# Selective-scan layer of a four-layer network: the product with B moves from TensorE and VectorE to GpSimd, and the side work is cut into evenly spaced items

## The chip, the cores and the metric

The kernel runs on one core of one Trainium2 chip, all in fp32. The metric is device time in microseconds of one launch. A core has five engines that run their own instruction queues in order: PE (TensorE), DVE (VectorE), ACT (ScalarE), POOL (GpSimd) and SP, which here only issues DMAs. They meet through semaphores.

## The reference

Four layers follow each other on four images of 128 channels and 48 x 48 pixels. Only layer 0 is changed; layers 1 to 3 (a deformable convolution, linear attention, two expert layers, softmax attention) stay as they are.

Layer 0 normalises the tokens, projects them to 256 channels, applies a depthwise 3 x 3 convolution and SiLU (call the result u), and then runs a selective scan in four directions k over the 2304 tokens, with 16 states n per channel:

```python
def step(h, inp):
    u_t, d_t, B_t, C_t = inp
    dA = jnp.exp(d_t[..., None] * A)
    h = h * dA + (d_t * u_t)[..., None] * B_t[:, :, None, :]
    y = jnp.einsum('bkdn,bkn->bkd', h, C_t)
    return (h, y)
```

Here d_t is a softplus of a small projection of u, and B_t and C_t are projections of u with one value per token and state. The four directions are summed, D * u is added, and the sum is normalised, gated with SiLU(z), projected back to 128 channels and added to the input.

## The kernel before, in words

**Tiling.** The 256 channels lie as two halves d of 128 partitions. The tokens of a direction are cut into three chunks of 768, so an image has 12 pieces (`PIECES`) and the four images have 48. A piece has 16 steps, one for each state n, so the loop at the end of `_layer0` runs over 768 steps g. The recurrence of one step is done by one scan instruction along the 768 tokens for each half (`scan`, L449).

**A step.** These are the operations, and the engine of each:
- `spread` (L415, L426): POOL makes dB, for each block of 128 tokens a diagonal matrix that holds B of this state (affine_select); SP loads rB, the same 768 values of B broadcast over all partitions, from DRAM.
- `decay` (L431): ACT makes dA = exp(delta * A) for each half.
- `times_b` (L435): PE multiplies duT (delta * u of half 0, turned to tokens by channels) with dB, twelve instructions here (six blocks; the profile counts two for each fp32 product), into the PSUM tile b0. This is the input of half 0.
- `scan` (L444, L449): DVE multiplies du of half 1 with rB into h, and then scans both halves: the first takes b0 from PSUM, the second h from SBUF, in place.
- `keep` (L461): POOL copies the last column of h as the start of the next chunk.
- `turn` (L467, L474): PE turns h to tokens by channels; ACT scales each token by C into hs.
- `back` (L482): PE turns hs back and adds it up over the 16 states in the PSUM tile yp.
- `collect` (L504, L513): after a piece, DVE adds yp to y in SBUF.

The steps are staggered: in step g the scan of g runs, `turn` and `back` of g - 1, `decay` and `times_b` of g + 1, `spread` of g + 2.

**Side work.** `prepare` makes delta, du, duT and the rows of B and C for the next piece (L321 to L393); `pre` normalises and convolves the next image (`before`, `convolve`), `post` finishes the last one (`after`, `offsets`), and `columns` (L282, POOL) copies u column by column. They stand in lists of closures, `urgent` and `others`. `fill` takes one or two from the front of them at three places of a step, so that the side work stands in the first half of a piece or so, and the list is emptied at some borders.

**What sets the order.** Instructions of PE, ACT, DVE and POOL are issued in the order of the code (`manual_schedule`), so each engine's queue holds the step's operations and the side work in the order in which this loop calls them. PSUM is shared by a pool of three tiles for all passing results, b0 (two banks) and yp (three banks). In SBUF most tiles have two buffers, rB three.

Of the kernel before, what the change touches and what calls it, by code (L numbers as in the profile page):

```python
# [23 lines left out]
P = 128  # L24
# [76 lines left out]
TPC = CH // P  # L101
HB = BLK // 2


def _layer0(ctx, env, dr, io, table, offs):
# [9 lines left out]
    ps = ctx.enter_context(tc.tile_pool(name="l0p", bufs=3, space=PSUM))  # L115
# [7 lines left out]
    def psum(*shape):  # L123
        return ps.tile(list(shape), F32, name="ps", tag="ps")
# [15 lines left out]
    bo = load("l1_bo", [NOFF, 1])  # L140

# [25 lines left out]

    b0 = py.tile([P, 2, 512], F32, name="b0").rearrange("p b f -> p (b f)")[:, :CH]
    yp = py.tile([P, ND * CH // 512, 512], F32, name="yp")
    yp = yp.rearrange("p b f -> p (b f)").rearrange("p (d f) -> p d f", d=ND)  # L170

    bank = [(d * CH + m * P) // 512 for m in range(TPC) for d in range(ND)]

# [3 lines left out]
    def taps(pp, weights, pad, r):  # L177

        for t in range(TAPS):
            nc.tensor.matmul(  # L180
                pp,
                weights[:, t, :],
                pad[:, 4 * r + t // 3 : 4 * r + t // 3 + 4, t % 3 : t % 3 + HW],
                start=t == 0,
                stop=t == TAPS - 1,
            )
# [4 lines left out]
    def standardise(x):  # L191
# [13 lines left out]
        def second():  # L205
            for g in range(G3):
                nc.vector.tensor_scalar(
                    x[:, g, :],
                    x[:, g, :],
                    mv[:, g, 0:1],  # L210
                    rstd[:, g : g + 1],
                    op0=ALU.subtract,
                    op1=ALU.mult,
                )
# [11 lines left out]

    def before(im, j):
# [8 lines left out]
        def turn():  # L236
            pt = psum(P, G3, C)
            for g in range(G3):
                nc.tensor.transpose(pt[:, g, :], t["xb"][:, bass.ts(g, P)], ident)
            t["xt"] = sp.tile([P, G3, C], F32, name="xt")  # L240
            nc.scalar.copy(t["xt"], pt)
            t["first"], t["second"] = standardise(t["xt"])

        def back():
            pt = psum(P, BLK)
            for g in range(G3):
                nc.tensor.transpose(pt[:, bass.ts(g, P)], t["xt"][:, g, :], ident)
            t["xn"] = sp.tile([P, BLK], F32, name="xn")
            nc.scalar.activation(t["xn"], pt, AF.Identity, bias=ln_b, scale=ln_g)
            nc.sync.dma_start(im.xn[:, cols], t["xn"])  # L250

        def project(d):
            pp = psum(P, BLK)
            nc.tensor.matmul(pp, ipT[:, bass.ts(d, P)], t["xn"], start=True, stop=True)
            nc.vector.tensor_copy(rows_of(pads[d], j), by_row(pp))
# [3 lines left out]
            turn,  # L259
            lambda: t["first"](),  # L260
            lambda: t["second"](),
            back,
            lambda: project(0),
            lambda: project(1),
        ]

    def convolve(d, r):

        pp = psum(P, HB)
        taps(pp, diag[:, d], pads[d], r)  # L270
        nc.scalar.activation(
            u_hw[:, d, bass.ts(r, HB)], pp, AF.Identity, bias=cb[:, d : d + 1]
        )
# [21 lines left out]

    def pre(im):
        steps = merged([before(im, j) for j in range(NBLK)], 3)
        convs = [lambda d=d, r=r: convolve(d, r) for r in range(L // HB) for d in range(ND)]
        return steps + convs + [activate]
# [8 lines left out]
    def prepare(x, before_it):  # L308
# [7 lines left out]
        def project(s):  # L316
            if s == 0:
                t["xd"] = sp.tile([NR + NS, CH], F32, name="xd", bufs=1)
            pp = psum(NR + NS, BLK)
            for d in range(ND):  # L320
                nc.tensor.matmul(  # L321
                    pp,
# [5 lines left out]
            nc.scalar.copy(t["xd"][:, bass.ts(s, BLK)], pp)  # L328
# [4 lines left out]
        def tokens():  # L333

            pp = psum(P, TPC, 2 * NS)
            for m in range(TPC):
                for d in range(ND):
                    nc.tensor.matmul(
                        pp[:, m, :],
# [4 lines left out]
                    )  # L344
            x.bc = sp.tile([P, TPC, 2 * NS], F32, name="bct")
            nc.vector.tensor_copy(x.bc, pp)


        def raw(s, d):
            if s == 0 and d == 0:  # L350
# [3 lines left out]
            pp = psum(P, BLK)  # L354
            nc.tensor.matmul(
                pp, dtT[:, k, bass.ts(d, P)], t["xd"][:NR, sub], start=True, stop=True
            )
            bias = dtb[:, d, k : k + 1]
            nc.scalar.activation(t["e"][:, d, sub], pp, AF.Abs, bias=bias)
            nc.vector.tensor_scalar(x.delta[:, d, sub], pp, bias, 0.0, op0=ALU.add, op1=ALU.max)  # L360

        def exps(d):
            nc.scalar.activation(t["e"][:, d, :], t["e"][:, d, :], AF.Exp, scale=-1.0)

        def rest(d):
            r = sp.tile([P, CH], F32, name=f"du{d}", bufs=1 + d)
            t["r", d] = r
            nc.vector.tensor_scalar(r, t["e"][:, d, :], 1.0, -1.0, op0=ALU.add, op1=ALU.add)
            nc.vector.scalar_tensor_tensor(
                r, r, -1.0, t["e"][:, d, :], op0=ALU.mult, op1=ALU.add  # L370
            )
# [4 lines left out]
        def total(d):  # L376
            dl = x.delta[:, d, :]
            nc.vector.tensor_add(dl, dl, t["e"][:, d, :])
            nc.vector.tensor_add(dl, dl, t["r", d])

        def inputs(d):

            nc.vector.tensor_mul(t["r", d], x.delta[:, d, :], u(d, 0, CH))
            if d:
                x.du1 = t["r", d]

        def turn(m0):
            if m0 == 0:
                x.duT = sp.tile([P, TPC, P], F32, name="duT")
            pt = psum(P, TPC // 2, P)  # L390
            for m in range(TPC // 2):
                nc.tensor.transpose(pt[:, m, :], t["r", 0][:, bass.ts(m0 + m, P)], ident)
            nc.scalar.copy(x.duT[:, m0 : m0 + TPC // 2, :], pt)  # L393

        def carry():
            x.last = x.at0 = None
# [4 lines left out]
        steps = [lambda s=s: project(s) for s in range(CH // BLK)]  # L401
        steps += [lambda s=s, d=d: raw(s, d) for s in range(CH // BLK) for d in range(ND)]
        steps += [lambda: exps(0), lambda: exps(1), tokens, lambda: rest(0)]
        steps += [lambda: rest(1), log, carry]
        steps += [lambda: total(0), lambda: inputs(0), lambda: total(1), lambda: turn(0)]
        steps += [lambda: inputs(1), lambda: turn(TPC // 2)]
        return steps
# [3 lines left out]
    def spread(x, n):  # L411

        x.dB = x.__dict__.get("dB", {})
        x.dB[n] = sp.tile([P, TPC, P], F32, name="dB")
        nc.gpsimd.affine_select(  # L415
            out=x.dB[n],
            in_=x.bc[:, :, n : n + 1].to_broadcast([P, TPC, P]),
            pattern=[[0, TPC], [1, P]],
            compare_op=ALU.is_equal,
            fill=0.0,  # L420
            base=0,
            channel_multiplier=-1,
        )
        x.rB = x.__dict__.get("rB", {})
        x.rB[n] = sp.tile([P, CH], F32, name="rB", bufs=3)
        nc.sync.dma_start(x.rB[n], x.rows[n : n + 1, :].to_broadcast([P, CH]))  # L426

# [5 lines left out]
    def times_b(x, n):  # L433
        for m in range(TPC):
            nc.tensor.matmul(  # L435
                b0[:, bass.ts(m, P)], x.duT[:, m, :], x.dB[n][:, m, :], start=True, stop=True
            )
        del x.dB[n]

    def scan(x, n, d):  # L440
        if d == 0:
            h = sp.tile([P, ND, CH], F32, name="h")
            x.__dict__.setdefault("h", {})[n] = h
            nc.vector.tensor_mul(h[:, 1, :], x.du1, x.rB.pop(n))  # L444
        h = x.h[n]
        out, b, da = h[:, d, :], h[:, 1, :] if d else b0, x.dA.pop((n, d))
        if x.k >= 2:
            out, b, da = out[:, ::-1], b[:, ::-1], da[:, ::-1]
        nc.vector.tensor_tensor_scan(  # L449
            out,  # L450
            da,
            b,
# [10 lines left out]
    def turn(x, n, m):  # L463
        if m % 2 == 0:
            x.tt = psum(P, 2, DI)
        for d in range(ND):
            nc.tensor.transpose(  # L467
                x.tt[:, m % 2, bass.ts(d, P)], x.h[n][:, d, bass.ts(m, P)], ident
            )
        if m % 2:  # L470
            for i in range(m - 1, m + 1):
                hs = sp.tile([P, DI], F32, name="hs", bufs=6)
                x.__dict__.setdefault("hs", {})[n, i] = hs
                nc.scalar.activation(  # L474
                    hs, x.tt[:, i % 2, :], AF.Copy, scale=x.bc[:, i, NS + n : NS + n + 1]
                )

    def back(x, n, m):
        hs = x.hs.pop((n, m))
        for d in range(ND):  # L480
            i = m * ND + d
            nc.tensor.matmul(  # L482
                yp[:, d, bass.ts(m, P)],
                hs[:, bass.ts(d, P)],
                ident,
                is_transpose=True,
                start=n == 0 and bank[i] not in bank[:i],
                stop=n == NS - 1 and bank[i] not in bank[i + 1 :],
            )
        if m == TPC - 1:  # L490
            del x.h[n]

    def collect(x):

        for d in range(ND):
            if x.k % 2:
                w0 = x.c * (CH // HW)
# [1556 lines left out]
```

## Time and profile before

| what | value |
|---|---|
| median of 3 runs | 13097.88 us (13094.8 to 13100.77) |
| the profiled execution, its own time | 13194.59 us |
| its span | 13192.9 us |
| mean granted TensorE clock | 0.927 |
| busy in the span | PE 11767.6, DVE 8201.4, ACT 6886.8, POOL 3474.9 us |
| scan of half 0 / half 1, where a carry comes in | 1811 / 1795 ns mean |
| first scan starts, last scan starts | 199.0 us, 5298.0 us |

An execution with the profiler on is not one of the three timed runs; its span is what all durations here come from. In rows of groups, a line names the source line, the engine, the operation, the tile written and the tiles read, the shapes and the count; behind the bar stand the busy time in us, the mean of one in ns, and how long the engine stood idle before these instructions, with what ended the wait. In a timeline the first number is the start in us from the start of the span and the second the duration in us. PE's ends are modelled and overlap, so its busy time overstates it.

### The profile page before, as it was taken

The page shows a single profiled execution, that of the slowest core. Times are in us where ns is not written, and L with a number is a line of the kernel's source. Part 1 is how long each engine was busy: PE and PEld are TensorE (multiplying, and loading weights), DVE is VectorE, ACT ScalarE, POOL GpSimd, SP SyncE. Part 2 cuts the span into 40 slices and gives each one's busy share as a digit, 9 for nine tenths or more (in the row PEclk, how much of TensorE's full clock was granted, in tenths as well). Part 3 has the DMA queues.
Part 4 walks back from the last instruction along what each step waited for, and adds up shares of the span by engine and source line. Part 5 has one row for each costly group of instructions (what it writes and reads, how often), then busy time and mean ns, then how long its engine had stood idle before and what let it go on. Part 6 is the DMA issues. An engine that isn't in the chain of part 4 may idle for free.

```text
span 13192.9 us, 198033 instructions
## 1 busy us (share of the span) xinstructions
PE 11767.6 (89%) x75384; PEld 9255.6 (70%) x75384; DVE 8201.4 (62%) x14751; ACT 6886.8 (52%) x13099; POOL 3474.9 (26%) x3957
## 2 busy tenths in 40 slices
PE   6888888888988888688799999999999988899989
PEld 5777677767776777588677777777777777433338
DVE  4878777877787788444456565666665651444441
ACT  4767766777677677211155565555555651222330
POOL 1212221222122222366443333333333320000000
PEclk8999999999999999899799999999999995799985
DMA  2212222122222222456400000000000003000012
GB/s 105 71 60 67 74 76 63 64 78 76 64 65 78 76 69 71 124 172 176 126 1 4 2 4 3 3 4 2 4 4 1 1 24 94 7 7 7 8 31 91
DMA packets 358291, 677.84 MB, mean 51 GB/s; under 512 B 40388, under 2 KB 195800, under 8 KB 355296
## 3 DMA queue, kind: packets, MB, share of 16 engines
q1 hardware_dynamic: 304464, 493.50, 11.9%
q0 software_dynamic: 51840, 169.91, 4.5%
q8 instruction: 599, 9.81, 0.3%
q14 instruction: 348, 2.85, 0.1%
q10 hardware_dynamic: 1040, 1.77, 0.0%
HBM read 602.63 MB, written 71.85 MB: 51 GB/s over the span
## 4 chain that ended last, share of the span: by engine, by line
PE 46%; DVE 6%; ACT 3%; issue 1%; POOL 0%; DMA 0%; another core or an unknown queue 0%; SPq 0%; ACTq 0%; DVEq 0%; POOLq 0%
PE pt L808 4%; PE psum L1284 4%; PE psum L1276 4%; PE pc L1170 3%; PE psum L1220 3%; PE scT L1757 3%; PE sc L1703 3%; PE out L1786 3%; PE psum L1190 2%; PE psum L1030 2%; PE psum L1031 2%; PE psum L1531 2%; PE psum L1516 2%; PE psum L964 2%; PE psum L1108 1%
## 5 line engine op out<-in xcount | busy, mean ns | idle before, releaser
L474 ACT ACTIVATE hs<-ps,bct 128x256 f32<-128x256 f32 x4608 | 1863.2, 480 | 498.2 <-PE ps L467 487.1
L482 PE MATMUL yp<-ident,hs 128*128 128x128 f32 x9216 | 1571.9, 289 | 263.0 <-ACT hs L474 260.0
L482 PEld LDWEIGHTS yp<-ident,hs 128*128 128x128 f32 x9216 | 1079.5, 145 | 567.2 <-ACT hs L474 521.5
L431 ACT ACTIVATE dA<-delta,l_Al 128x768 f32<-128x768 f32 x1536 | 1464.0, 953 | 0.9
L435 PE MATMUL b<-dB,duT 128*128 128x128 f32 x9216 | 1236.1, 287 | 254.9 <-DVE h L449 254.5
L435 PEld LDWEIGHTS b<-dB,duT 128*128 128x128 f32 x9216 | 1159.1, 202 | 293.6 <-issue 263.4
L467 PE MATMUL ps<-ident,h 128*128 128x128 f32 x9216 | 1320.4, 280 | 41.3 <-DVE delta L360 27.1
L467 PEld LDWEIGHTS ps<-ident,h 128*128 128x128 f32 x9216 | 1084.5, 144 | 144.0 <-issue 61.2
L415 POOL TENSOR_SCALAR_AFFINE_SELECT dB<-bct 128x768 f32<-128x768 f32 x768 | 706.6, 920 | 1770.6 <-PE b L435 1609.2
L449 DVE TENSOR_TENSOR_SCAN h<-dA,carry,b 128x768 f32<-128x768 f32 x512 | 927.1, 1811 | 67.3 <-PE b L435 37.9
L449 DVE TENSOR_TENSOR_SCAN h<-dA,carry,h 128x768 f32<-128x768 f32 x512 | 919.2, 1795 | 0.0
L461 POOL COPY carry<-h 128x2 f32<-128x2 f32 x512 | 308.7, 603 | 2052.5 <-DVE h L449 1830.8
L1765 ACT ACTIVATE pT<-scT 128x768 f32<-128x768 f32 (+2 forms) x504 | 378.1, 750 | 896.8 <-PE scT L1757 892.1
L808 PE MATMUL pt<-ident,gw 128*128 128x128 f32 x5184 | 679.8, 292 | 152.7 <-DVE gw L802 124.7
L444 DVE TENSOR_TENSOR h<-du,rB 128x768 f32<-128x768 f32 x768 | 735.0, 957 | 115.3 <-issue 100.9
L1024 POOL TENSOR_TENSOR T<-T,bias 128x384 f32<-128x384 f32 x384 | 384.4, 1001 | 1560.9 <-DVE fn L952 1520.7
L808 PEld LDWEIGHTS pt<-ident,gw 128*128 128x128 f32 x5184 | 644.7, 205 | 182.8 <-DVE gw L802 119.0
L795 POOL DMA_INDIRECT g<-table,idx x648 | 656.1, 1012 | 403.5 <-DVE gw L802 184.4
L802 DVE TENSOR_TENSOR gw<-g,wq 128x512 f32<-128x512 f32 x648 | 426.2, 692 | 497.3 <-PE pt L808 429.5
L1713 DVE TENSOR_REDUCE mx<-sc 128x2 f32<-128x1024 f32 (+3 forms) x400 | 428.4, 1071 | 363.6 <-PE sc L1703 358.5
L1284 PE MATMUL psum<-w,gl 128*128 128x128 f32 x4608 | 546.2, 275 | 1.8 <-ACT wqsq L1037 1.5
L1284 PEld LDWEIGHTS psum<-w,gl 128*128 128x128 f32 x4608 | 530.6, 192 | 3.1 <-ACT wqsq L1037 2.3
(332 smaller groups left out, 23377.4 us busy)
## 6 DMA issues: line engine op xcount, KB each, us to landing
rB<-rows SPq DMA_DIRECT2D x768, 384.0 KB
w<-f_w SPq DMA_DIRECT2D x16, 2048.0 KB
w<-f_w SPq DMA_DIRECT2D x128, 256.0 KB
table<-y SPq DMA_DIRECT2D x9, 2304.0 KB
table<-tok SPq DMA_DIRECT2D x16, 1152.0 KB
g<-table,idx POOLq DMA_INDIRECT x648
xb<-x SPq DMA_DIRECT2D x48, 192.0 KB
xn<-xn SPq DMA_DIRECT2D x48, 192.0 KB
```

Of the source, the lines that this page charges most:

```text
L415: nc.gpsimd.affine_select(out=x.dB[n], in_=x.bc[:, :, n : n + 1].to_broadcast([P, TPC, P]), pattern=[[0, TPC], [1, P]], compare_op=ALU.is_ ...
L431: nc.scalar.activation(dA, x.delta[:, d, :], AF.Exp, scale=A[:, d, x.k, n : n + 1])
L435: nc.tensor.matmul(b0[:, bass.ts(m, P)], x.duT[:, m, :], x.dB[n][:, m, :], start=True, stop=True)
L444: nc.vector.tensor_mul(h[:, 1, :], x.du1, x.rB.pop(n))
L449: nc.vector.tensor_tensor_scan(out, da, b, initial=0.0 if x.before is None else x.before.carry[:, d, n : n + 1], op0=ALU.mult, op1=ALU.add,)
L467: nc.tensor.transpose(x.tt[:, m % 2, bass.ts(d, P)], x.h[n][:, d, bass.ts(m, P)], ident)
L474: nc.scalar.activation(hs, x.tt[:, i % 2, :], AF.Copy, scale=x.bc[:, i, NS + n : NS + n + 1])
L482: nc.tensor.matmul(yp[:, d, bass.ts(m, P)], hs[:, bass.ts(d, P)], ident, is_transpose=True, start=n == 0 and bank[i] not in bank[:i], stop ...
L795: nc.gpsimd.indirect_dma_start(out=g, out_offset=None, in_=table, in_offset=bass.IndirectOffsetOnAxis(ap=idx[:, j : j + 1], axis=0),)
L808: nc.tensor.matmul(pt[:, t - t0, :], gw[:, q, :], ident, start=q == 0, stop=q == 3)
L1276: nc.tensor.matmul(pg, y.w["w1"][:, bass.ts(f, P)], t["uT"], start=True, stop=True)
L1284: nc.tensor.matmul(pp[:, g, :], t["gl"][:, f, bass.ts(g, P)], y.w["w2"][:, f, :], start=f == 0, stop=f == DFF // P - 1,)
```

## The change

`AHEAD = 2`, `HBUF = 4`. The whole product du * B, of both halves, is made by POOL, two steps before its scan, into the tile h, which has four buffers in place of two. Both scans then work in place on h. dB, duT, b0 and the matmuls of `times_b` are gone. rB is loaded three steps ahead; `keep` is called one step later.

```diff
     def spread(x, n):
-        x.dB[n] = sp.tile([P, TPC, P], F32, name="dB")
-        nc.gpsimd.affine_select(
...
         x.rB[n] = sp.tile([P, CH], F32, name="rB", bufs=3)
         nc.sync.dma_start(x.rB[n], x.rows[n : n + 1, :].to_broadcast([P, CH]))
+
+    def times_b(x, n):
+        h = sp.tile([P, ND, CH], F32, name="h", bufs=HBUF)
+        x.__dict__.setdefault("h", {})[n] = h
+        for d in range(ND):
+            nc.gpsimd.tensor_mul(h[:, d, :], x.du[:, d, :], x.rB[n])
+        del x.rB[n]
...
     def scan(x, n, d):
-        if d == 0:
-            h = sp.tile([P, ND, CH], F32, name="h")
-            x.__dict__.setdefault("h", {})[n] = h
-            nc.vector.tensor_mul(h[:, 1, :], x.du1, x.rB.pop(n))
-        h = x.h[n]
-        out, b, da = h[:, d, :], h[:, 1, :] if d else b0, x.dA.pop((n, d))
+        h, da = x.h[n][:, d, :], x.dA.pop((n, d))
...
         nc.vector.tensor_tensor_scan(
-            out,
+            h,
             da,
-            b,
+            h,
```

In `prepare`, `raw` is cut into a matmul and `parts`: the absolute value is no longer made by ACT (Abs) but by DVE, and `rounded` and the second half of `standardise` (`second`) are two-input forms in place of tensor_scalar. The turns of du fall away.

```diff
-            nc.scalar.activation(t["e"][:, d, sub], pp, AF.Abs, bias=bias)
-            nc.vector.tensor_scalar(x.delta[:, d, sub], pp, bias, 0.0, op0=ALU.add, op1=ALU.max)
+            nc.vector.tensor_scalar(dl, pp, bias, 0.0, op0=ALU.add, op1=ALU.max)
+
+            nc.vector.scalar_tensor_tensor(
+                t["e"][:, d, sub], dl, -2.0, pp, op0=ALU.mult, op1=ALU.add
+            )
...
-            nc.vector.tensor_scalar(r, t["e"][:, d, :], 1.0, -1.0, op0=ALU.add, op1=ALU.add)
...
+            nc.vector.scalar_tensor_tensor(
+                x.du[:, d, :],
+                t["e"][:, d, :],
+                1.0,
+                one.to_broadcast([P, CH]),
+                op0=ALU.add,
+                op1=ALU.subtract,
+            )
```

yp is laid out by pairs of token blocks. A new `take` copies each third of it with ACT into the SBUF tile ys as soon as it is done, and `collect` adds from ys. The PSUM pool of three is split: two tiles for `turn` (ps), two for the side work of images (pf), one for `prepare` (pu).

All side work is cut into items that ask one engine or two: a matmul group is one item, the operation that empties its PSUM tile the next; a convolution of nine taps is three items and an output. They stand in lanes: a `Lane` spreads its items evenly over a fixed number of places, three places to a step.

```diff
+    class Lane:
+        def __init__(self, items, places):
+            self.items, self.places, self.at, self.done = items, places, 0, 0
+
+        def go(self):
+            self.at += 1
+            while self.done * self.places < len(self.items) * min(self.at, self.places):
+                self.items[self.done]()
+                self.done += 1
...
+            if n == 0 and i + 1 < len(pieces):
+                lanes["next"] = Lane(prepare(pieces[i + 1], pieces[i]), 3 * (NS - AHEAD) - 1)
...
+                lanes["image"] = Lane(items, 3 * (5 * NS - 3))
+            if (p, n) == (5, 0) and b + 1 < NB:
+                lanes["image"] = Lane(pre(images[b + 1]), 3 * 6 * NS)
...
+            fill()
+            do(spread, g + AHEAD + 1)
+            do(times_b, g + AHEAD)
             do(scan, g, 0)
             do(scan, g, 1)
-            do(keep, g)
+            do(keep, g - 1)
+            do(turn, g - 1, 0)
+            do(back, g - 2, 2)
...
             do(decay, g + 1, 0)
...
+            fill()
+            do(turn, g - 1, 1)
+            do(back, g - 1, 0)
...
+            do(decay, g + 1, 1)
+            fill()
+            do(turn, g - 1, 2)
             do(back, g - 1, 1)
```

## The prediction

> **What bounds the kernel now.** I read the sums by stretch first, to see how much of the span the change can reach. The loop over the 768 scan steps is the stretch 199 to 5300 us; columns are PE, PEld, DVE, ACT, POOL busy, clock, DMA share, GB/s.
>
> ```profile
> 199.00:5300.00 5101.00, 4429.12 (x32365) 3780.09 (x32364) 4133.54 (x3552) 3682.49 (x7075) 1095.96 (x1350) 0.96 0.22 70
> ```
>
> 5101 us / 768 = 6.64 us per step. Per step DVE works 5.38, ACT 4.79, POOL 1.43 us. PE's 4429 us are spans that overlap (eight weight loads of L467 stand in 0.86 us in the timeline of a step, so 36 need 3.9 us). DVE is the fullest engine, yet it idles 967 us (1.26 per step). The timeline of DVE shows that there are two kinds of step. In a quiet step, with no work of the next piece in it, DVE is full:
>
> ```profile
> 2062.36 0.93 DVE L444 TENSOR_TENSOR h<-du,rB 128x768 f32<-128x768 f32 x1
> 2063.21 1.80 DVE L449 TENSOR_TENSOR_SCAN h<-dA,carry,b 128x768 f32<-128x768 f32 x1
> 2064.93 1.78 DVE L449 TENSOR_TENSOR_SCAN h<-dA,carry,h 128x768 f32<-128x768 f32 x1
> 2066.64 0.93 DVE L444 TENSOR_TENSOR h<-du,rB 128x768 f32<-128x768 f32 x1
> ```
>
> Starts lie 0.85, 1.72 and 1.71 apart: 4.28 us. The other steps carry the preparation and take longer, because DVE stands in line for results that ACT and PE have only just been asked for. The waits of DVE in the loop (us in total, times, longest):
>
> ```profile
> DVE delta L360 <- ACT e L359: 170.6, 63, 11.3
> DVE bct L346 <- PE ps L338: 154.3, 47, 7.1
> DVE y L513 <- PE yp L482: 153.0, 35, 9.8
> DVE ft L626 <- PE ps L624: 113.4, 18, 7.3
> ```
>
> Last I looked at GpSimd beside DVE, since the change sets the two to work together. At 1711 us GpSimd ran two copies of one size, alone in its queue; first its lines, then DVE's:
>
> ```profile
> 1711.67 1.49 POOL L282 COPY u_wh<-u_hw 128x768 f32<-128x768 f32 x1
> 1713.10 2.97 POOL L282 COPY u_wh<-u_hw 128x768 f32<-128x768 f32 x1
> ```
>
> ```profile
> 1712.56 2.22 DVE L449 TENSOR_TENSOR_SCAN h<-dA,carry,h 128x768 f32<-128x768 f32 x1
> ```
>
> The scan (dA and h both in SBUF) starts while the first copy runs; it takes 2.22 in place of 1.79 and ends at 1714.78, 1.62 after the copy's end at 1713.16. The second copy starts inside the scan, takes 2.97 in place of 1.49 and ends 1.29 after the scan. Each waited for the other's end. The same trio stands at 3044 and 4365 us. With the scan of the first half (b in PSUM, one SBUF input) it is otherwise: the selects of L415 that start inside it keep their clean 0.87. Beside a product with two SBUF inputs the select waits, and the next product then waits for the select:
>
> ```profile
> 2048.20 1.43 POOL L415 TENSOR_SCALAR_AFFINE_SELECT dB<-bct 128x768 f32<-128x768 f32 x1 [8.11 <-PE b L435]
> ```
>
> ```profile
> 2047.97 0.93 DVE L383 TENSOR_TENSOR du<-delta,u_wh 128x768 f32<-128x768 f32 x1
> 2048.82 1.61 DVE L444 TENSOR_TENSOR h<-du,rB 128x768 f32<-128x768 f32 x1
> ```
>
> The select ends 0.73 after du's end (2048.90), and h ends 0.80 after the select's. So turns alternate, one instruction each, and about 0.15 of each start-up hides under the other's end.
>
> **What the Trainium skill says.** "SBUF — State Buffer", section "Who interferes with whom": a DVE instruction with two SBUF inputs contends with a GpSimd instruction that reads SBUF, for the whole instruction, and the later one fully blocks; with at most one SBUF input, outside the two-port modes, it doesn't. The trace agrees in both halves: 2.97 and 2.22 above, 0.87 beside b in PSUM. "GPSIMD Engine Reference", section "Elementwise — side-by-side cycle accounting": an fp32 product on GpSimd costs about twice DVE's (4497 ns for 2048 elements). The trace has the price:
>
> ```profile
> L1024 POOL TENSOR_TENSOR T<-T,bias 128x384 f32<-128x384 f32 x384 | 384.4, 1001 | 1560.9 <-DVE fn L952 1520.7 <-ACT bias L1020 22.4 <-DVE rstd L944 1.9
> L969 POOL TENSOR_TENSOR dk<-dk,tok_b 128x2304 f32<-128x2304 f32 x1 | 5.0, 5048 | 14.5 <-DMA tok_b<-l_tok_b 14.5
> ```
>
> (5048 - 1001) / 1920 = 2.11 ns an element, so 1.81 us for 768. "Perfetto Trace Analysis", section "Optimizing Scalar/DVE Operations", warns that moving work between these two engines might not help. No row here shows a two-input GpSimd product beside a scan; the copies are the nearest.
>
> **The change part by part.**
>
> Removed. The product with B on TensorE: 12 matmuls and 12 weight loads a step, the select (0.87 on POOL), the turns of du into duT. PE isn't what ends a step here, so this is worth only the waits "DVE h <- PE b", 65 us in all. DVE loses L444: 767 x 0.86 (spacing) = 660 us. ACT loses the Abs, 188 x 0.581 = 109 us, and the duT copies, 94 x 0.485 = 46.
>
> Added on DVE. The second half of `parts` is a scalar_tensor_tensor from PSUM, 192 x about 0.62 (the row of L360, same shape and source) = 119 us; it has one SBUF input, so it can run while GpSimd holds the pair. `rounded` is a two-input form for a tensor_scalar: 96 x (0.96 - 0.54) = 40 us. `second`: 144 small operations, at most 0.2 more each, 29 us. DVE's own work becomes (4134 - 660 + 188) / 768 = 4.77 us a step.
>
> Added on ACT: `take`, 144 copies of 512 elements from PSUM at 0.589 (row yt<-ps 128x512) = 85 us; ACT becomes (3682 - 155 + 85) / 768 = 4.70.
>
> Added on POOL: 1536 products of 1.81 us = 3.62 a step. Both scans now have two SBUF inputs, since the first half no longer comes from PSUM. This is the step that decides. A scan and a product can't overlap beyond the start-up, so what counts per step is the sum of all work that needs the shared interface:
> - two scans at 1.62 (the time after a GpSimd end, above): 3.24
> - two products at 1.81 - 0.14 = 1.67: 3.34
> - per piece ten two-input DVE operations of 768 (`rounded`, `rest`, four `total`, `inputs`) at 0.96 - 0.15 = 0.81, and two `collect`, now from SBUF, at 1.325 - 0.15 = 1.17: 10.4 / 16 = 0.65
> - per image `gated`, `second`, and on POOL the columns, pow and pad copies: 24 x 0.8 + 144 x 0.3 + 24 x 1.3 + 48 x 0.7 + 24 x 0.4 = 137 us / 768 = 0.18
> - `keep`, 512 x 0.19 (its shortest; most of its mean 0.603 was waiting) / 768 = 0.13
>
> Sum 7.54 us a step, x 768 = 5790 us against 5101: +690.
>
> Moved. `keep` goes one step later and stands behind two products in POOL's queue; its reader is the next piece's first scan of that state, 15 steps on, so nothing waits. pow and the pad copies stand behind the products too, up to about 7 us; DVE's `second` and PE's taps then wait, but while they wait GpSimd uses the interface, so the sum isn't raised. The rB loads on SP's queue are issued three steps ahead in place of two, with the same three buffers: free since the product of that state ended. At no cost: the split into items at equal distances, the PSUM pools of two, two and one in place of three, a PSUM tile of its own for each third of `turn`. What hides their waits is the interface itself: DVE, ACT and PE have 2.8 us a step to spare. For the same reason the even spacing brings nothing: the 1.26 us a step that DVE idled is filled by waiting for GpSimd. Without that cover they would show as in the rival below. Prologue and tail (199 and 130 us) keep their chains: 0 to 10 us.
>
> The profiled execution took 13194.6 us (span 13192.9), 96.7 more than the median 13097.9. 13194.6 + 690 = 13885 profiled, 13788 against the median; I say 13785.
>
> Both ends of the unknown, the handoffs: if the write end of a product overlaps a scan as well, 0.5 less: 7.0 x 768 = 5376, +275, 13373. If nothing overlaps, 1.79 and 1.81 in full, 7.54 + 0.64 = 8.2: 6298, +1197, 14295. Below nothing is excluded in this case, since 7.0 is above 6.64.
>
> **The rivals.**
> - *Products run beside scans* (faster). Place: the shared interface. For: no row shows a two-input product of GpSimd against a scan, and 2.11 ns an element leaves its reads gaps. Then DVE (4.77) and ACT (4.70) bound the step; at 92% full, as DVE in quiet steps of 4.5 to 4.6 us, 5.2: 768 x 5.2 = 3994, -1107: 11990. It decides from the point where 0.9 of the 6.58 us of scans and products overlap (7.54 - 6.64). Against: the three trios, and two additions of 384 at 10844 us, GpSimd's T<-T,bias (1.24 for 1.00) and DVE's T<-r,eT (1.24 for 0.55), which blocked each other.
> - *Fixed places turn into waits on top*: an item that comes due before its input stalls an in-order engine while GpSimd too has run out of free h buffers (four). If all of the old 1.26 comes back so: 8.8 a step, 6758, +1657: 14755. Against: GpSimd has two steps of lead and work for 3.6 us of each.
> - *Blocking only in part*, near the break-even of 6.64: 13098. The change then wins on DVE what it loses in turns.
>
> **How the numbers follow.** Forecast 0.80, within 13370 to 14295; waits on top 0.05; products beside scans 0.11; in part 0.04 (0.01 faster, 0.02 within 0.2%, 0.01 slower). 0.2% is about what a measurement of this kernel can tell from no change. Slower 0.80 + 0.05 + 0.01 = 0.86, same 0.02, faster 0.12. The range is the forecast's own: 0.80.
>
> **What would show it.** Right: a loop of about 5790 us; scans of some 3.3 us mean in place of 1.79, in both halves; products of some 3.3 in place of 1.8; POOL busy for nine tenths of the loop, PE down to some 55% ((4429 - 1234) / 5790, 1234 being the row of L435); steps alike near 7.5, with no quiet steps of 4.5. Wrong: scans that keep 1.75 to 1.8 beside products, or steps of 5 to 6 us; products much under 1.7 alone; DVE idle behind ACT or PE while POOL is idle too.

## The result and the profile after

The changed kernel takes 13716.23 us (median of 4 runs, 13708.95 to 13723.42), the kernel before 13096.34 on the same chip: a ratio of 1.0473, 95% interval 1.0455 to 1.0491, or 620 us more. The prediction said 13785, +690 in the loop, with a range of 13370 to 14295. Sign, mechanism and size hold, and the size is 70 us too high.

The stretch from the first scan's start to the last scan's end, in the profile after (columns as before: PE, PEld, DVE, ACT, POOL busy, granted clock, DMA share, GB/s):

```profile
195.90:5927.80 5731.90, 4035.82 (x22873) 3220.55 (x22873) 5541.57 (x2974) 3609.11 (x6922) 5058.26 (x2125) 0.80 0.19 62
```

5731.9 / 768 = 7.46 us a step, against 6.64: +631 us. DVE is busy 97% of it and idles 190 us where it idled 967. POOL is busy 88%. So both engines look full at once, though DVE issues fewer instructions than before (2974 against 3552). The rest of the profiled span is 113 us shorter than before's (13711.1 - 5731.9 = 7979 against 8092), which is the 97 us by which before's profiled execution stood above its median, and little else.

A stretch of the timeline after, one instruction a line, first DVE and then POOL, shows what the busy time is made of:

```profile
2063.94 1.75 DVE L496 TENSOR_TENSOR_SCAN h<-dA,h 128x768 f32<-128x768 f32 x1
2065.61 3.30 DVE L496 TENSOR_TENSOR_SCAN h<-dA,h 128x768 f32<-128x768 f32 x1
2068.83 3.30 DVE L496 TENSOR_TENSOR_SCAN h<-dA,h 128x768 f32<-128x768 f32 x1
2072.06 1.73 DVE L496 TENSOR_TENSOR_SCAN h<-dA,h 128x768 f32<-128x768 f32 x1
```

```profile
2064.14 3.15 POOL L484 TENSOR_TENSOR h<-du,rB 128x768 f32<-128x768 f32 x1
2067.26 3.26 POOL L484 TENSOR_TENSOR h<-du,rB 128x768 f32<-128x768 f32 x1
2070.46 1.65 POOL L508 COPY carry<-h 128x2 f32<-128x2 f32 x1
2072.20 3.19 POOL L484 TENSOR_TENSOR h<-du,rB 128x768 f32<-128x768 f32 x1
```

Add start and duration to read the ends. DVE's first scan ends at 2065.69, POOL's product at 2067.29 (1.60 later), the next scan at 2068.91 (1.62 later), the next product at 2070.52 (1.61), the next scan at 2072.13 (1.61), the copy of two columns with it. One instruction at a time moves, one from each engine by turns, about 1.6 us each, and a span of 3.3 is half waiting. The first scan kept 1.75, for the turn before it was short: POOL was at a copy of two columns that ended at 2064.07, 1.62 before the scan's end. A busy share of 97% here does not mean that DVE works 97% of the time.

The groups over the whole profile after:

```profile
L484 POOL TENSOR_TENSOR h<-du,rB 128x768 f32<-128x768 f32 x1536 | 4297.2, 2821 | 676.9 <-PE ps L515 306.4
L496 DVE TENSOR_TENSOR_SCAN h<-dA,carry,h 128x768 f32<-128x768 f32 x1024 | 2670.3, 2655 | 98.9 <-ACT dA L490 87.8
L496 DVE TENSOR_TENSOR_SCAN h<-dA,h 128x768 f32<-128x768 f32 x512 | 1303.7, 2592 | 49.8 <-ACT dA L490 42.0
L508 POOL COPY carry<-h 128x2 f32<-128x2 f32 x512 | 674.8, 1318 | 0.0
```

The scans' mean is 2.6 us in both halves, but no typical scan takes 2.6: counted one by one and rounded to a tenth, 551 of the 1536 lie at 1.7 or 1.8 and 763 at 3.3 or 3.4. All 763 began beside a product. Of the 551, 296 began in the last moment of a copy of two columns, and 225 found POOL idle. The products have three groups: 191 at 1.8, 267 at 2.5 (begun beside a shorter DVE instruction), 625 at 3.3; the rest lie between.

The waits in the loop (us in total, times, longest) have left DVE and stand behind it:

```profile
DVE h L496 <- ACT dA L490: 129.8, 87, 6.1
```

```profile
ACT hs L521 <- PE ps L515: 1855.3, 834, 10.4
PE ps L515 <- DVE h L496: 1005.9, 490, 7.3
POOL h L484 <- PE ps L515: 306.4, 93, 8.1
```

ACT waits for PE, PE waits for the scan. POOL runs ahead until it finds no free h buffer, which PE gives back only after the scan.

### The profile page after: what moved, and what is told of

Read it like the earlier page. It is cut to its first block, busy times and chain, and to the rows that moved or that the text cites. A ratio compares the mean times of both kernels' runs of the same rounds, so it can differ in the third digit from the quotient of the medians.

```text
span 13711.1 us, 178311 instructions
## 1 busy us (share of the span) xinstructions
PE 11338.7 (83%) x65880; PEld 8645.9 (63%) x65880; DVE 9629.2 (70%) x14176; ACT 6813.8 (50%) x12943; POOL 7473.7 (55%) x4725
## 3 DMA queue, kind: packets, MB, share of 16 engines
q1 hardware_dynamic: 304464, 493.50, 11.2%
q14 instruction: 344, 2.82, 0.1%
## 4 chain that ended last, share of the span: by engine, by line
PE 39%; DVE 6%; ACT 2%; issue 2%; POOL 2%; DMA 2%; SPq 0%; ACTq 0%; DVEq 0%; POOLq 0%
PE psum L1383 4%; PE psum L1375 4%; PE pc L1269 3%; PE psum L1319 3%; PE scT L1856 3%; PE sc L1802 2%; PE out L1885 2%; PE psum L1289 2%; POOL g L894 2%; PE psum L1129 2%; PE psum L1130 2%; PE psum L1630 2%; PE psum L1615 2%; PE psum L1063 1%; DMA g<-table,idx 1%
## 5 line engine op out<-in xcount | busy, mean ns | idle before, releaser
L484 POOL TENSOR_TENSOR h<-du,rB 128x768 f32<-128x768 f32 x1536 | 4297.2, 2821 | 676.9 <-PE ps L515 306.4
L496 DVE TENSOR_TENSOR_SCAN h<-dA,carry,h 128x768 f32<-128x768 f32 x1024 | 2670.3, 2655 | 98.9 <-ACT dA L490 87.8
L515 PE MATMUL ps<-ident,h 128*128 128x128 f32 x9216 | 1838.2, 326 | 1007.2 <-DVE h L496 1005.9
L515 PEld LDWEIGHTS ps<-ident,h 128*128 128x128 f32 x9216 | 1350.2, 170 | 1380.8 <-DVE h L496 715.5
L529 PE MATMUL yp<-ident,hs 128*128 128x128 f32 x9216 | 1811.0, 324 | 246.4 <-ACT hs L521 191.9
L529 PEld LDWEIGHTS yp<-ident,hs 128*128 128x128 f32 x9216 | 1321.2, 168 | 457.5 <-ACT hs L521 338.3
L496 DVE TENSOR_TENSOR_SCAN h<-dA,h 128x768 f32<-128x768 f32 x512 | 1303.7, 2592 | 49.8 <-ACT dA L490 42.0
L508 POOL COPY carry<-h 128x2 f32<-128x2 f32 x512 | 674.8, 1318 | 0.0
L1138 POOL TENSOR_TENSOR wk<-wk,r 128x384 f32<-128x384 f32 x192 | 190.7, 993 | 883.6 <-DVE r L1137 880.6
L1209 DVE TENSOR_REDUCE kmax<-psum 128x8 f32<-128x352 f32 x576 | 273.7, 520 | 402.8 <-ACT dk L1208 397.7
```

Of the source, the lines that this page charges most:

```text
L484: nc.gpsimd.tensor_mul(h[:, d, :], x.du[:, d, :], x.rB[n])
L496: nc.vector.tensor_tensor_scan(h, da, h, initial=0.0 if x.before is None else x.before.carry[:, d, n : n + 1], op0=ALU.mult, op1=ALU.add,)
L508: nc.gpsimd.tensor_copy(x.carry[:, :, n : n + 1], x.h[n][:, :, end : end + 1])
L515: nc.tensor.transpose(tt[:, m, bass.ts(d, P)], x.h[n][:, d, bass.ts(2 * q + m, P)], ident)
L529: nc.tensor.matmul(yp[:, q, (2 * d + m) * P : (2 * d + m + 1) * P], hs[:, bass.ts(d, P)], ident, is_transpose=True, start=n == 0 and m == ...
```

## The experiments

Eleven kernels. They ran in groups, each group on a chip of its own beside the kernel before (13216.76 us for the first four, 13096.75 for the next four, 13090.62 for the two after them, 13221.39 for the last), so ratios are compared; where loops of different groups are set side by side below, the ratios give about the same difference. The theory is the prediction's, that GpSimd's products and DVE's two-input work exclude each other. The rivals: GpSimd's product is late and DVE waits for its data; the split items and their fixed places cost the time; GpSimd at work slows DVE whatever it does. "Loop" is the stretch from first to last scan in the profiled execution.

| kernel | ratio to before (95%) | loop, us | DVE busy |
|---|---|---|---|
| before | 1 | 5101 | 4134 |
| after | 1.0473 (1.0455 to 1.0491) | 5732 | 5542 |
| product on DVE | 1.0049 (1.0032 to 1.0066) | 5154 | 4839 |
| half on GpSimd | 1.0479 (1.0461 to 1.0496) | 5738 | 5320 |
| third product | 1.1411 (1.1392 to 1.1430) | 6978 | 6017 |
| before, even places | 0.9947 (0.9930 to 0.9964) | 5040 | 4155 |
| writes only | 1.0046 (1.0029 to 1.0063) | 5172 | 4842 |
| unread product | 1.0797 (1.0779 to 1.0815) | 6142 | 5865 |
| half, late on DVE | 1.0285 (1.0268 to 1.0303) | 5474 | 5297 |
| items, old product | 1.0520 (1.0502 to 1.0538) | 5712 | 4220 |
| product under scan 0 | 1.0162 (1.0148 to 1.0176) | 5331 | 3647 |
| its order alone | 1.0306 (1.0292 to 1.0320) | 5520 | 4159 |
| product under scan 0, old order | 0.9903 (0.9887 to 0.9920) | 4995 | 3819 |

### Does the place of the product decide?

**Product on DVE.** One word of the kernel after is changed; nothing else.

```diff
-            nc.gpsimd.tensor_mul(h[:, d, :], x.du[:, d, :], x.rB[n])
+            nc.vector.tensor_mul(h[:, d, :], x.du[:, d, :], x.rB[n])
```

> The changed kernel with both halves of the product with B on DVE in place of GpSimd; all else is as in the changed kernel. Theory (scans and GpSimd products take turns at one interface): the two products cost DVE 2 x 0.86 us of spacing and take 2 x 1.67 of turns away, so a step falls from 7.46 to about 6.5 us (DVE's own work: scans 3.44, products 1.72, the rest 1.25), loop about 5000 us, time about 12980 (12900 to 13250); scans are back at 1.73 to 1.8 us each. Rival (the finer items, the fixed places or the split PSUM pools cost the time): the loop stays within 100 us of 5732, time 13600 to 13750.

Ratio 1.0049: nine tenths of the loss is gone with GpSimd's products (0.0473 - 0.0049 = 0.0424 of 0.0473). The scans are clean again, though DVE now makes 1536 products besides:

```profile
L496 DVE TENSOR_TENSOR_SCAN h<-dA,carry,h 128x768 f32<-128x768 f32 x1024 | 1808.9, 1808 | 0.0
L496 DVE TENSOR_TENSOR_SCAN h<-dA,h 128x768 f32<-128x768 f32 x512 | 875.0, 1749 | 0.0
```

The time expected was missed, 12980 against 13280. DVE's own work is 4839 / 768 = 6.30 us a step, and DVE idles 0.41 more, most of it ahead of its products (263 us), which stand two steps early in its queue. For 146 us of this the trace names PE, which frees the h buffers, for the rest no engine. From this kernel DVE's work without any product comes out at 6.30 - 2 x 0.86 = 4.58 (the prediction had 4.77).

**Third product.** Half 1's product is made twice on GpSimd with the same operands, so only the work is more.

```diff
             nc.gpsimd.tensor_mul(h[:, d, :], x.du[:, d, :], x.rB[n])
+        nc.gpsimd.tensor_mul(h[:, 1, :], x.du[:, 1, :], x.rB[n])
```

> The changed kernel with the product of half 1 made twice on GpSimd, three products a step. Theory of turns: one more turn of 1.67 us a step, 768 x 1.67 = +1280 us, less what of it falls into times when DVE doesn't want the interface (GpSimd idles 674 us of the loop): 14600 to 15000. Rival (GpSimd and DVE overlap, and something else bounds the loop): GpSimd's own work of 3 x 1.81 = 5.4 us fits into the step of 7.46, so the time stays at 13716 within 1%.

The loop grows by 6978 - 5732 = 1246 us, 1.62 us for each of 768 products: the whole turn, as the sum of the interface says (1.67). POOL is then busy 6760 of 6978 us, and the theory without exclusion, which saw room on POOL, is out. Late data plays a part in this kernel too: DVE idles 961 us, 730 of them ahead of scans whose products aren't ready.

**Half on GpSimd.** Half 0's product goes to DVE, at the same place two steps ahead. If only the sum over the interface counted, 1.67 - 0.81 a step would be saved.

```diff
-        for d in range(ND):
-            nc.gpsimd.tensor_mul(h[:, d, :], x.du[:, d, :], x.rB[n])
+        nc.vector.tensor_mul(h[:, 0, :], x.du[:, 0, :], x.rB[n])
+        nc.gpsimd.tensor_mul(h[:, 1, :], x.du[:, 1, :], x.rB[n])
```

> The changed kernel with half 0 of the product on DVE and half 1 on GpSimd. Theory of turns: one product at 1.67 us is replaced by one at 0.81 to 0.86, step 7.46 - 0.83 = 6.6 us, loop about 5090, time about 13070; scans fall into two groups, near 1.75 and near 3.3 us, the long ones fewer than half as many as before. Rival (GpSimd is only too slow, with both products 3.6 us of work for a step plus its queue, and overlaps with DVE): with half of its work gone DVE's own 5.6 us bound the step, loop about 4350, time about 12330. Rival (items and places): no change, 13716.

A clear miss: 1.0479, no better than after (a step 0.8 us shorter was expected), though only 403 scans are doubled in place of 763. DVE's busy time is 5320 / 768 = 6.93 a step; its own work is 4.58 + 0.86 = 5.44, so it is blocked 1.49 us a step by one product. The other 0.54 is idle, and nearly all of it before its own product (L483 here), which stands two steps ahead and holds up the scans queued behind it. For the first of these rows the trace names PE, which frees the h buffers, for the second no engine:

```profile
DVE h L483 <- PE ps L515: 196.6, 70, 5.3
DVE h L483 <- issue: 185.0, 96, 5.0
```

**Half, late on DVE.** The same split, with DVE's product just ahead of the scan that reads it, and a fourth rB buffer for it.

```diff
-        x.rB[n] = sp.tile([P, CH], F32, name="rB", bufs=3)
+        x.rB[n] = sp.tile([P, CH], F32, name="rB", bufs=4)
...
-        for d in range(ND):
-            nc.gpsimd.tensor_mul(h[:, d, :], x.du[:, d, :], x.rB[n])
-        del x.rB[n]
+        nc.gpsimd.tensor_mul(h[:, 1, :], x.du[:, 1, :], x.rB[n])
...
+        if d == 0:
+            nc.vector.tensor_mul(x.h[n][:, 0, :], x.du[:, 0, :], x.rB.pop(n))
```

> Half 1 of the product on GpSimd two steps ahead, half 0 on DVE, but just before its own scan in place of two steps ahead. In the run with half on GpSimd DVE stood idle 404 us of the loop of 5738, 382 of them in front of its product, waiting for a free h buffer. Theory: that wait ate the gain; here it is gone, loop about 5400 to 5500, ratio 1.022 to 1.030. Rival (a GpSimd product costs the same however many there are): loop stays at 5700 or more, ratio 1.045 or more.

1.0285, as expected. The idle time falls from 418 to 178 us and the loop to 5474, so the early place had cost that idle time. Blocking stays: 5297 / 768 - 5.44 = 1.46 us a step. So with DVE's queue in order, one GpSimd product costs DVE 1.5 us, and DVE makes the same product in 0.86. That is why even half of the change is a loss.

### What of the product blocks?

Two kernels set idle work on GpSimd beside "product on DVE", into a tile that nobody reads. They tell data dependence, occupation and reading apart.

**Unread product** and **writes only**:

```diff
+        nc.gpsimd.tensor_mul(scratch, x.du[:, 1, :], x.rB[n])
```

```diff
+        for _ in range(5):
+            nc.gpsimd.memset(scratch, 0.0)
```

> The kernel with both products on DVE (ratio 1.0049, loop 5154) with one more product a step on GpSimd, which reads du and rB and writes a scratch tile that nobody reads: GpSimd's reading alone, without any data that anyone waits for. Theory of turns: each of the 768 products takes 1.3 to 1.67 us from DVE, +1000 to +1280 us, ratio 1.08 to 1.10, with scans near 3.3 us. Rival (the scans of the changed kernel wait for the data of late products): nobody waits for this one, so the ratio stays near 1.005.

> The kernel with both products on DVE with five GpSimd memsets of 768 columns a step into a scratch tile, about 3.3 us of GpSimd work a step that writes SBUF and reads nothing; nobody reads the tile. Theory of turns at the shared read interface: no cost, ratio 1.005 within 0.005, scans at 1.73 to 1.81 us. Rival (any GpSimd access to SBUF takes turns with DVE): each step grows by up to 3.3 us, ratio 1.05 to 1.2.

The unread product costs (6142 - 5154) / 768 = 1.29 us a step, at the lower edge of what was expected. It comes as DVE's busy time (+1026 us), not as idle, and 252 scans lie at 3.3 to 3.4. No DVE instruction waits for its result. The memsets keep POOL busy longer, 3415 us of the loop against 2350, and cost nothing that can be told from none: a ratio of 1.0046 against 1.0049, a loop 18 us longer. In the timeline of "writes only", two scans (L499 there) lie beside the memsets at their clean 1.76 each, DVE's line first:

```profile
2064.24 3.52 DVE L499 TENSOR_TENSOR_SCAN h<-dA,carry,h 128x768 f32<-128x768 f32 x2
```

```profile
2063.38 3.92 POOL L487 MEMSET scratch<- 128x768 f32 x5
```

So it is GpSimd's reads that take turns with DVE's second input, not its being at work. This is what the Trainium skill states in "SBUF — State Buffer", section "Who interferes with whom": contention is with a GpSimd instruction that reads SBUF, not with one that only writes it. The unchanged ratio agrees.

### What is the even spacing worth alone?

**Before, even places.** The kernel before with lanes: its own unsplit items at equal distances in place of the lists emptied from the front.

```diff
-            fill(n % 2)
+            if n == 0 and i + 1 < len(pieces):
+                lanes["next"] = Lane(prepare(pieces[i + 1], pieces[i]), 3 * (NS - 2) - 1)
+            if (p, n) == (0, 3) and b < NB:
...
+                lanes["image"] = Lane(items, 3 * (5 * NS - 3))
+            if (p, n) == (5, 0) and b + 1 < NB:
+                lanes["image"] = Lane(pre(images[b + 1]), 3 * 6 * NS)
+            fill()
...
-            fill(True)
+            fill()
```

> The kernel before with the side work in evenly spaced lanes, but with its own items (a matmul and what empties its PSUM tile in one item), its PSUM pool of three and its product on PE and DVE: the even spacing alone. Theory of turns: the interface is little used here, so the spacing can only take away waits of DVE (967 us of the loop of 5101); if half of them go, loop about 4600, time about 12600 (12450 to 12950). Rival (even spacing costs time in itself, since items stand between the operations of every step): slower than before, 13200 or more.

0.9947: it helps, by half a percent and not by the five expected. DVE's idle time in the loop only falls from 967 to 885 us. The waits come in more and shorter pieces:

```profile
DVE delta L360 <- ACT e L359: 202.1, 101, 5.4
DVE bct L346 <- PE ps L338: 180.3, 47, 7.6
```

Before, the first was 170.6 us in 63 waits, the longest 11.3. These fit an item that asks ACT and then DVE for the same data, and so makes DVE wait for the chain inside it wherever the item stands; this was not tried apart.

**Items, old product.** The kernel after with its split items, but the product as before: half 0 by PE into b0, half 1 by DVE; Abs goes back to ACT, and the two-input forms become one-input forms again. b0 takes two banks of PSUM, so each of the split pools keeps one tile.

```diff
-    ps = ctx.enter_context(tc.tile_pool(name="l0p", bufs=2, space=PSUM))
-    pf = ctx.enter_context(tc.tile_pool(name="l0f", bufs=2, space=PSUM))
+    ps = ctx.enter_context(tc.tile_pool(name="l0p", bufs=1, space=PSUM))
+    pf = ctx.enter_context(tc.tile_pool(name="l0f", bufs=1, space=PSUM))
...
-        for d in range(ND):
-            nc.gpsimd.tensor_mul(h[:, d, :], x.du[:, d, :], x.rB[n])
+        for m in range(TPC):
+            nc.tensor.matmul(
+                b0[:, bass.ts(m, P)], x.duT[:, m, :], x.dB[n][:, m, :], start=True, stop=True
+            )
```

> The changed kernel's lanes and one-engine items with the product of the kernel before: half 0 on PE into PSUM, half 1 on DVE; ABS back on ACT, one-input forms back; one PSUM tile each for the turns, the image items and the piece items, since b0 takes two banks. Theory (the product's place made the change slow, the items took DVE's waits away): DVE's work falls to about 4839 - 657 - 104 = 4080 us, idle 200 to 350, loop about 4350, ratio about 0.943 (0.93 to 0.965). Rival (items and places don't help, or a single PSUM tile makes PE and ACT wait for each other): ratio 0.98 or more.

1.0520, the rival's case. The scans are clean (1.80 and 1.79 us), but with one tile PE and ACT wait for each other in turn:

```profile
ACT hs L542 <- PE ps L536: 1811.0, 1581, 6.2
PEld ps L536 <- ACT hs L542: 928.4, 1148, 5.5
PE ps L536 <- ACT hs L542: 625.0, 1025, 5.2
```

With b0 in place only one bank is left for the turns. That this costs the time fits the waits above, but it was not tried apart. What splitting is worth by itself was therefore not measured.

### Can GpSimd make a product at no cost?

The skill's same section says that a DVE instruction with at most one SBUF input, outside the two-port modes, doesn't contend. The scan of half 0 in the kernel before is one: b comes from PSUM. Three kernels start from "before, even places".

**Product under scan 0** puts half 1's product on GpSimd one step ahead and DVE in the order scan 0, side work, scan 1; **its order alone** has that order with the product on DVE ahead of scan 1. Both call `keep` a step later and give h three buffers.

```diff
+    def times_b1(x, n):
+        h = sp.tile([P, ND, CH], F32, name="h", bufs=3)
+        x.__dict__.setdefault("h", {})[n] = h
+        nc.gpsimd.tensor_mul(h[:, 1, :], x.du1, x.rB.pop(n))
...
-            fill()
-            do(spread, g + 2)
             do(scan, g, 0)
-            do(scan, g, 1)
-            do(keep, g)
+            do(keep, g - 1)
+            do(times_b1, g + 1)
+            fill()
+            do(spread, g + 2)
...
+            fill()
+            do(scan, g, 1)
```

> The kernel before with even places (ratio 0.9947, loop 5040, DVE busy 4155, idle 885), half 0 still on PE into PSUM, but half 1's product on GpSimd one step ahead, and DVE's order turned: the scan of half 0, then the side work, then the scan of half 1, so that GpSimd's product comes free at the end of the scan of half 1 and runs beside the scan that reads PSUM. Theory (only operations with two SBUF inputs take turns): the product costs DVE nearly nothing there, DVE's work falls by 767 x 0.86 = 660 us, waits for turns add at most 230, loop 4400 to 4750, ratio 0.945 to 0.975; scans of half 0 stay at 1.75 to 1.81. Rival (every scan takes turns with GpSimd): 1.67 - 0.86 = 0.8 us a step more than on DVE, ratio 1.03 or more, scans of half 0 near 3.3. Rival (PE or ACT bound the loop once DVE is relieved): ratio 0.98 to 1.0 with clean scans.

> The same kernel and the same order of DVE (scan of half 0, side work, scan of half 1), with half 1's product on DVE just before its scan: the order without the move. Theory: DVE's work is as with even places, the order is of little weight, ratio 0.985 to 1.005. Rival (the order makes the gain of the run beside it): ratio as low as there.

The mechanism works: the scans of half 0 keep 1.80 and 1.74 us mean, and products fall from 2.82 to 1.95. 465 of the 768 scans of half 0 lie beside a product for more than 0.4 us, and none takes over 1.82; of the scans of half 1, 209 do, and they take 2.20 on average and up to 3.46. A product and a scan of half 0, each at its clean length, side by side:

```profile
2072.91 1.81 POOL L443 TENSOR_TENSOR h<-du,rB 128x768 f32<-128x768 f32 x1
```

```profile
2073.99 1.81 DVE L450 TENSOR_TENSOR_SCAN h<-dA,carry,b 128x768 f32<-128x768 f32 x1 [1.29 <-PE b L435]
```

Yet the kernel is slower than before, 1.0162 where 0.945 to 0.975 was expected. The second run says why: the order alone takes the ratio from 0.9947 to 1.0306 (expected near 1, and missed), and the move gains 13491.7 - 13306.9 = 185 us back. With the scans apart, DVE waits more for ACT and PE. In "its order alone":

```profile
DVE delta L360 <- ACT e L359: 400.8, 142, 6.6
DVE bct L346 <- PE ps L338: 289.7, 47, 9.7
DVE h L450 <- PE b L435: 279.6, 164, 5.2
```

In "before, even places" these three are 202, 180 and 83 us. With the move, the wait for b alone rises from 280 to 613 us.

**Product under scan 0, old order** keeps the order of before; the product, issued ahead of the step's first fill, begins when the copy of the carry behind the last step's scan 1 is done.

```diff
+            do(times_b1, g + 1)
             fill()
             do(spread, g + 2)
             do(scan, g, 0)
             do(scan, g, 1)
```

> The kernel before with its side work at even places, in its own order of VectorE's instructions, and half 1's product put on GpSimd alone, one step ahead, so that it begins when the scans of the step before end. Theory: most of the loss of the run with the late scan came from its order, and a scan that reads its second operand from PSUM doesn't take turns with GpSimd. Moving the product between the two runs with that order gained 185 us; here the product should lie beside scan 0, which reads PSUM, so VectorE loses some 660 us of work, while the waits for PSUM and for ScalarE take part of it back: 12700 to 12950, a ratio of 0.970 to 0.988 to the kernel before, below the 0.9947 of the same kernel with the product on VectorE. Rival: the product slips to where scan 1 and the side items run, they take turns, and the ratio is 0.995 to 1.02.

0.9903, the fastest of all, though between the two ranges expected. Of the 660 us that DVE no longer spends in products, its busy time keeps 337 (4155 - 3819): the products still slip onto other work of DVE at times. The scans of half 1 take 1.96 and 1.84 us on average where they took 1.80 and 1.73, some 114 us in all, and operations of `prepare` and `standardise` some 250 us more. One-input operations are among these: the first step of `rest`, from SBUF to SBUF, first in "before, even places" and then here:

```profile
L368 DVE TENSOR_SCALAR du<-e 128x768 f32<-128x768 f32 x94 | 54.2, 576 | 0.0
```

```profile
L368 DVE TENSOR_SCALAR du<-e 128x768 f32<-128x768 f32 x94 | 106.8, 1137 | 0.0
```

The one-input operation of L360, whose input lies in PSUM, keeps its 0.61. So one SBUF input isn't always enough to be free of GpSimd. The exception in the skill's sentence, the two-port modes, would fit; no run here tests which mode L368 is in.

Of these 337 us the loop keeps 45. The rest is idle, most of it in one wait:

```profile
DVE h L450 <- PE b L435: 384.8, 256, 5.7
```

which is 83 us in "before, even places". The idle time grows by 292 us and this wait by 302, so what DVE gained it now waits for PE's half of the product. Whether an earlier b would free it was not tried.

## Why the prediction was right

**What bounds the kernel, and the handoff.** The trios of copies and scans gave 1.62 for a scan after a GpSimd end. In the kernel after, 969 scans had a product of POOL end within their span, and all but three of them ended 1.6 to 1.7 us after that end; of 1378 products within which a DVE instruction with two SBUF inputs ended, 1376 ended 1.5 to 1.7 after it. The products that met nothing took 1.79 to 1.83. The price of 1.81 came from additions on GpSimd, in the trace as on the page that the prediction cites, and was taken over to products; it fits them. The terms 1.62, 1.67 and 1.81 hold to 0.1 us, and so does the judgment that a product excludes a scan as a copy does.

**The sum.** 7.54 a step forecast, 7.46 measured. DVE's clean work was put at 4.77 and is 4.58; ACT's at 4.70, and is 3609 / 768 = 4.70. One small term failed. `keep` was costed at 0.19 us each, its shortest time, and takes 1.32 on average: an instruction of two columns also waits its turn. Its read holds the interface only briefly (above, the copy ended with the scan ahead), so the sum bore it.

**What the sum means.** The sum asks how long the shared interface is held, and this can be counted: in the kernel after, a POOL instruction that reads or a DVE instruction with two SBUF inputs is under way for 5649 of the loop's 5732 us, 7.36 a step. Only 0.11 a step is free, so the interface is what bounds this kernel. The forecast of 7.54 was 0.18 too much for it and left out the free time; these two errors cancel in part. In "third product" the same count gives 6947 of 6978 us, 9.05 a step: 1.69 more for a term of 1.67. "Half on GpSimd" shows where the sum isn't enough: the interface is held 6.69 a step, near the 6.6 expected, but 0.78 a step is free and the step is as long. DVE's in-order queue decides as well. Seen from DVE, a step of the kernel after is 4.58 of its own work, 2.64 blocked (7.22 busy less 4.58) and 0.25 idle.

**Steps alike near 7.5.** This failed. The distance between first scans is under 4.9 us in a tenth of the steps and over 11.2 in another, and its mean by state runs from 4.9 to 11.8. Counted by state, a step of 4.9 us on average sees 1.2 products begin, one of 11.8 us sees 3.2: POOL fills the long steps with products, then stands without a free h buffer (306 us of waiting for PE), and the steps that follow run with fewer. The time of a piece is steadier instead: 113 to 131 us, where it was 89 to 152 before. The scans' mean was forecast at 3.3 and is 2.6: the forecast let every scan stand behind a whole product. But 296 scans stand behind a copy of two columns, 225 find POOL idle, and some products meet other work of DVE.

**PE at 55%.** It is 70%. The count of matmuls fell as said (32365 to 22873), but the spans of those that stayed grew: a turn of h takes 326 ns on average where it took 280, at a granted clock of 0.80 in the loop for 0.96. DVE waits for PE only 0.5 us in the whole loop.

**Even spacing brings nothing.** Not shown for this change, since no kernel has GpSimd's products with the old lists. DVE's idle time of 967 us is 190 now, but blocking is not the only way to that: in "product on DVE", with the same lanes and split items, no products on GpSimd and a fuller DVE, it is 315. With unsplit items the lanes bring 0.5%, and the idle time stays at 885.

**The rivals.** Products beside scans: out by "third product" and "unread product". Waits on top: DVE idles only 0.25. In part: a scan in three keeps 1.75, but through timing, since those that met a product ended a full 1.6 us behind it. If a product's 2.11 ns an element leaves gaps in its reads, no scan got through them. The subtraction of 97 us for before's own execution was right: after's profiled span, 13711.1, lies at its median.

## What to carry to other kernels

Before moving an operation from VectorE to an idle GpSimd, ask what VectorE has under way meanwhile: if it reads two SBUF tiles, GpSimd's reads are paid on VectorE, here 1.3 to 1.6 us for a product that VectorE itself makes in 0.86. Some operations with one SBUF input pay as well, so look at the spans of each. Moved work is worth something beside instructions that read one operand from PSUM, if the order of the queue stays and the next wait (here PE's b) is short. And two engines near 100% busy may be one interface in turns: compare ends, and compare a span with the same instruction alone.

## What was not expected of the hardware

The granted TensorE clock was lower where PE had less to do in a us. With the same 22870 matmuls in the loop it was 0.85 in 5154 us ("product on DVE"), 0.80 in 5732 (after), 0.79 in 6142 ("unread product") and 0.75 in 6978 ("third product"); with 32364 in 5040 us ("before, even places") it was 0.98. Fewer matmuls in a us went with a lower clock in these five. But "items, old product" had 0.96 with 32356 in 5712 us, and "its order alone", with as many in a shorter loop of 5520, had 0.92. So more than the mean rate plays a part; what sets the clock was not tried.
